# The first mixture's second layer, with an expert's slots along the columns

## The chip, the cores and the metric

The kernel runs on one core of one Trainium2 chip. Its engines work side by side, each on its own stream of instructions: TensorE (PE; its weight loads are listed as PEld), VectorE (DVE), ScalarE (ACT), GpSimd (POOL) and SyncE (SP), which here only issues transfers. The time is the device time of one launch in microseconds, the median of several runs.

## The reference

Two layers of a recurrent model run on x of 8 sequences x 512 tokens x 128 features. Each layer computes x + s * silu(g) from xn = layernorm(x): s comes from a sequence branch, g from a mixture of experts.

- In the first layer s is a state-space block (convolution, a scan over 512 tokens with 16 states of 256 channels, a small MLP). The mixture has 24 experts and picks two per token. Capacity is 86 rows per expert in each of four groups of tokens. With combine weights w and dispatch d in {0, 1}:

```
hidden = sum_e w[s,e] * ( xn[s] @ W1[e] + b1[e] )      128 -> 512
hidden = relu(layernorm(hidden))                        one weight set per group
out    = sum_e w[s,e] * ( hidden[s] @ W2[e] + b2[e] )  512 -> 128
g      = layernorm(out + xn)
```

- In the second layer s is causal attention with 8 heads, g a mixture of 128 experts.

The change touches only the first mixture.

## The kernel before

**Slots.** The routing (`routing`, L336) gives each row that an expert takes a slot: 4 x 86 = 344 rows, kept as three tiles of 128 slots, so `SLOTS` is 384 (L29, L30). `inv[p, c, e]` holds the token of slot p of tile c, `wsl` its combine weight (0 for an empty slot). `row` holds, for a token, the two slots at which it finds its experts' rows.

**The mixture** is three loops (`mixture`, near the end of `tile_kernel`), each over experts or pairs of token tiles.

1. `expert1` (L439): per tile, gather 128 rows of xn by `inv` (GpSimd, L445), transpose them (L446), and copy the three transposes out (L448). Then per tile two products into one PSUM tile, the bias (a product of a one-hot column `pick` with `bias`, which holds b1 and b2 split into three bf16 parts, L452) and the rows times W1 (L453). ScalarE scales by `wsl` into `hs` (L454), and one store per expert writes 384 rows of 2 KB to `hs_dram` (L455).
2. `between` (L457): per token tile, two gathers from `hs_dram`, their sum, a layer norm, and a store to `hid_dram`.
3. `expert2` (L506): per tile, gather 128 rows of 512 from `hid_dram` (L512), four transposes (L515), Relu into `hgT` (L517), a bias product (L518), and four products that accumulate (L520): hidden is the stationary operand, W2 the moving one, so slots lie on the partitions of the result `po`. ScalarE scales by `wsl` into `os` (L521). One store per expert goes to `os_dram` (L522).

**Order of the work.** The mixture runs beside the state-space branch (`front`, `scan`, `back`): for 64 steps of the mixture 20 steps of the scan are put between them in the source. A scan step has VectorE scans (L612), ScalarE exponentials (L608) and 16 transposes on TensorE (L616). The framework then sets each engine's static order by its own planner, so that in the trace transposes of one tile stand among products of another. `weights` (L426) loads an expert's matrix up to three experts ahead on SP's queue. The stores `hs` and `os` are on the same queue. Gathers are issued by GpSimd. After the mixture, `after` (L524) gathers from `os_dram`, so it waits for its stores.

**Buffers.** PSUM tiles of the mixture share a pool of four banks (`ps_e`, tag "pe"). In SBUF `hg`, `hs` and `hd` share four buffers (tag "big"); `xTe`/`hgT`, `os`, `lw` and `lb` have two each.

Of the kernel before, what the change touches and what calls it, by code (L numbers as in the profile page):

```python
# [8 lines left out]
F32 = mybir.dt.float32  # L9
I32 = mybir.dt.int32  # L10
BF16 = mybir.dt.bfloat16
U32 = mybir.dt.uint32
AF = mybir.ActivationFunctionType
# [7 lines left out]
P = 128  # L21
B, L, D = 8, 512, 128
NJ = L // P
# [3 lines left out]
KC = 4  # L27
E0, C0, DH, H0 = 24, 86, 512, 4

SG, CP = 3, 128  # L30
SLOTS = SG * CP
E1, C1 = 128, 32
S1 = E1 * C1
HEADS, DHEAD = 8, 128
# [12 lines left out]
def tile_kernel(ctx: ExitStack, tc: tile.TileContext, t: dict, out: bass.AP):  # L47
    nc = tc.nc
    V, S, G, T, Q = nc.vector, nc.scalar, nc.gpsimd, nc.tensor, nc.sync
# [6 lines left out]
    def load(src, shape, name, pool=None, dtype=F32):  # L56
        tl = (pool or const).tile(list(shape), dtype, name=name, tag=name)
        Q.dma_start(tl, src)
        return tl

    ident = const.tile([P, P], F32, name="ident")
# [22 lines left out]
    xn_dram = dram.tile([NTOK, D], F32, name="xn_dram")  # L84
    xT_dram = [dram.tile([P, L], F32, name=f"xT_dram{b}") for b in range(B)]
    xd_dram = [dram.tile([DTR + 2 * DS, L], F32, name=f"xd_dram{b}") for b in range(B)]
    hs_dram = dram.tile([E0 * SLOTS, DH], F32, name="hs_dram")
    hid_dram = dram.tile([NTOK, DH], F32, name="hid_dram")
    os_dram = dram.tile([E0 * SLOTS, D], F32, name="os_dram")

# [7 lines left out]
    def bc(ap, shape):  # L98
        return ap.to_broadcast(list(shape))
# [26 lines left out]
    def gather(dst, table, idx):  # L126
        G.indirect_dma_start(dst, None, table[:, :], IOA(idx, 0))  # L127
# [29 lines left out]
    ps_m = pool(ssm, "ps_m", 2, "left", space=PSUM)  # L157
# [31 lines left out]
    inv_pool = pool(moe, "inv_pool", 1, "right")  # L189
# [1 line left out]
    wsl = inv_pool.tile([CP, SG, E0], F32, name="wsl")  # L191


    bias = inv_pool.tile([3 * 32, DH + D], BF16, name="bias")
    zero = inv_pool.tile([P, L], F32, name="zero")
    G.memset(zero, 0.0)
    pick = inv_pool.tile([3 * 32, E0], BF16, name="pick")
# [3 lines left out]
    rt = pool(rt_ctx, "rt", 1, "right")  # L201
# [93 lines left out]
    lno_w = load(t["lno_w"].partition_broadcast(P), (P, D), "lno_w", w3)  # L295
    lno_b = load(t["lno_b"].partition_broadcast(P), (P, D), "lno_b", w3)

    eb = xp.tile([3 * 32, DH + D], F32, name="eb", bufs=1)
    G.memset(eb, 0.0)
    for k in range(3):  # L300
        Q.dma_start(eb[32 * k : 32 * k + E0, 0:DH], t["eb1"])
        Q.dma_start(eb[32 * k : 32 * k + E0, DH:], t["eb2"])
    part = xp.tile([3 * 32, DH + D], BF16, name="part", bufs=1)
    for k in range(3):
        ks = slice(32 * k, 32 * k + 32)
        G.tensor_copy(part, eb)
# [112 lines left out]
            )  # L419


    def chosen(e):

        return bc(pick[:, e : e + 1], (3 * 32, CP))

    def weights(shape, source):  # L426

# [11 lines left out]
    def expert1(e, w):  # L439

        we = w(e)
        px = ps_e.tile([P, SG, CP], F32, name="px", tag="pe")
        for c in range(SG):
            xg = me.tile([CP, D], F32, name="xg", bufs=8)
            gather(xg, xn_dram, inv[:, c, e : e + 1])  # L445
            T.transpose(px[:, c, :], xg, ident[:CP, :CP])  # L446
        xT = me.tile([P, SG, CP], F32, name="xTe", tag="xTe")
        S.copy(xT, px)  # L448
        hs = me.tile([CP, SG, DH], F32, name="hs", tag="big", bufs=4)
        for c in range(SG):  # L450
            ph = ps_e.tile([CP, DH], F32, name="ph", tag="pe")
            T.matmul(ph, chosen(e), bias[:, 0:DH], start=True, stop=False)  # L452
            T.matmul(ph, xT[:, c, :], we, start=False, stop=True)  # L453
            S.activation(hs[:, c, :], ph, AF.Copy, scale=wsl[:, c, e : e + 1])  # L454
        Q.dma_start(hs_dram[e * SLOTS : (e + 1) * SLOTS, :].rearrange("(c p) f -> p c f", p=CP), hs)  # L455

    def between():  # L457


        n = 2  # L460
        pairs = [(h, b0) for h in range(H0) for b0 in range(0, B, n)]
        begun, affine = [], []

        def begin(h, b0):
            if b0 == 0:
                lw = me.tile([P, DH], F32, name="lw")
                Q.dma_start(lw, t["lnh_w"][h].partition_broadcast(P))
                lb = me.tile([P, DH], F32, name="lb")
                Q.dma_start(lb, t["lnh_b"][h].partition_broadcast(P))
                affine.append((lw, lb))  # L470
            hd = me.tile([P, n, 2, DH], F32, name="hd", tag="big", bufs=4)
            for j in range(n):
                for k in range(2):
                    gather(hd[:, j, k, :], hs_dram, row[:, h * B + b0 + j, k : k + 1])
            begun.append(hd)

        for pair in pairs[:3]:
            begin(*pair)
        for i, (h, b0) in enumerate(pairs):
            if i + 3 < len(pairs):  # L480
                begin(*pairs[i + 3])
            hd, (lw, lb) = begun[i], affine[h]
            mean = st.tile([P, n], F32, name="lnh_m")
            var = st.tile([P, n], F32, name="lnh_v")
            for j in range(n):
                V.scalar_tensor_tensor(
                    hd[:, j, 0, :], hd[:, j, 0, :], 1.0, hd[:, j, 1, :], ALU.mult, ALU.add,
                    accum_out=mean[:, j : j + 1],
                )
            V.tensor_scalar(mean, mean, -1.0 / DH, None, ALU.mult)  # L490
            for j in range(n):
                S.activation(
                    hd[:, j, 1, :], hd[:, j, 0, :], AF.Square, bias=mean[:, j : j + 1],
                    accum_out=var[:, j : j + 1],
                )
            S.activation(var, var, AF.Sqrt, bias=eps6, scale=1.0 / DH)
            V.reciprocal(var, var)
            for j in range(n):
                x = hd[:, j, 0, :]
                V.scalar_tensor_tensor(x, x, mean[:, j : j + 1], lw, ALU.add, ALU.mult)  # L500
                V.scalar_tensor_tensor(x, x, var[:, j : j + 1], lb, ALU.mult, ALU.add)
                g = order(h * B + b0 + j)
                Q.dma_start(hid_dram[g * P : (g + 1) * P, :], x)
            yield

    def expert2(e, w):  # L506
        we = w(e)
        po = ps_e.tile([CP, SG, D], F32, name="po", tag="pe")
        os = me.tile([CP, SG, D], F32, name="os", tag="o")
        hg = me.tile([CP, SG, DH], F32, name="hg", tag="big", bufs=4)  # L510
        for c in range(SG):
            gather(hg[:, c, :], hid_dram, inv[:, c, e : e + 1])  # L512
            pt = ps_e.tile([P, NJ, CP], F32, name="pht", tag="pe")
            for f in range(NJ):
                T.transpose(pt[:, f, :], hg[:, c, f * P : (f + 1) * P], ident[:CP, :CP])  # L515
            hT = me.tile([P, NJ, CP], F32, name="hgT", tag="xTe")
            S.activation(hT, pt, AF.Relu)  # L517
            T.matmul(po[:, c, :], chosen(e), bias[:, DH:], start=True, stop=False)  # L518
            for f in range(NJ):
                T.matmul(po[:, c, :], hT[:, f, :], we[:, f, :], start=False, stop=(f == NJ - 1))  # L520
            S.activation(os[:, c, :], po[:, c, :], AF.Copy, scale=wsl[:, c, e : e + 1])  # L521
        Q.dma_start(os_dram[e * SLOTS : (e + 1) * SLOTS, :].rearrange("(c p) f -> p c f", p=CP), os)  # L522

    def after(b):  # L524

# [652 lines left out]
```

## Time and profile before

| | us |
|---|---|
| median of 3 runs (1658.43 to 1661.57) | 1659.78 |
| profiled execution, its time | 1664.84 |
| profiled execution, its span | 1662.9 |
| first layer of the mixture (`expert1`) | 121 to 263 |
| normalisation (`between`) | 263 to 421 |
| second layer (`expert2`) | 421 to 604 |

| engine | busy us | share of the span | in 421 to 604 |
|---|---|---|---|
| TensorE | 1246.0 | 75% | 158.7 |
| VectorE | 1237.9 | 74% | 114.2 |
| ScalarE | 961.8 | 58% | 114.7 |
| GpSimd | 585.4 | 35% | 88.9 |

The mean granted TensorE clock is 0.87 of full speed. Busy time of TensorE is the sum of matmul lengths as recorded; matmuls overlap, so starts are the better measure of pace. The chain of work that ended last passes through many engines (VectorE 33%, TensorE 33%, DMA 11%, GpSimd 10% of the span).

### The profile page before, as it was taken

How to read it: one execution, taken by the hardware profiler on the slowest of the kernel's cores; microseconds unless marked ns; L12 is line 12 of the kernel's file. 1: busy time of each engine (PE TensorE's matmuls, PEld its weight loads, DVE VectorE, ACT ScalarE, POOL GpSimd, SP SyncE). 2: the span in 40 equal slices, each digit the busy share in tenths (PEclk: the TensorE clock that was granted, in tenths of full speed). 3: DMA queues.
4: the chain of work that ended last, by engine and by line, in shares of the span. 5: the costliest groups of instructions: out<-in, count | busy, mean ns of one | idle time of the engine just before them, and what ended most of it. 6: DMA issues, size and time to landing. Idle time of an engine off the chain costs nothing.

```text
span 1662.9 us, 20509 instructions
## 1 busy us (share of the span) xinstructions
PE 1246.0 (75%) x6797; PEld 870.4 (52%) x6797; DVE 1237.9 (74%) x2809; ACT 961.8 (58%) x1691; POOL 585.4 (35%) x502
## 2 busy tenths in 40 slices
PE   4788887501599874497779987887798898889763
PEld 2644444301587872254636664575476676567442
DVE  6558766578636863699979996999999999375454
ACT  2227666666367754555766676657676675552442
POOL 2005773553653537025250232215331102020365
PEclk9887998755799985688999998999899999999986
DMA  4438987766685742223232213223231120338143
GB/s 136 148 108 261 317 308 259 240 227 202 204 280 167 249 135 55 88 77 88 83 78 70 76 51 78 90 81 85 83 95 63 59 89 13 92 102 250 54 116 96
DMA packets 170668, 222.76 MB, mean 134 GB/s; under 512 B 15722, under 2 KB 115898, under 8 KB 170562
## 3 DMA queue, kind: packets, MB, share of 16 engines
q1 hardware_dynamic: 125634, 101.35, 19.5%
q0 software_dynamic: 26496, 52.98, 12.0%
q10 hardware_dynamic: 18432, 67.12, 12.0%
q8 instruction: 54, 0.88, 0.2%
q14 instruction: 52, 0.43, 0.1%
HBM read 163.52 MB, written 57.80 MB: 133 GB/s over the span
## 4 chain that ended last, share of the span: by engine, by line
DVE 33%; PE 33%; DMA 11%; POOL 10%; issue 8%; ACT 4%; another core or an unknown queue 1%; SPq 0%; POOLq 0%; DVEq 0%; ACTq 0%
DVE u L612 8%; PE sc L835 4%; PE po L862 4%; DVE u L613 3%; DVE u L610 3%; PE ph L453 3%; DVE sc L837 3%; POOL o L130 3%; DMA hd<-hs_dram,row 2%; PE py L616 2%; PE po L520 2%; DVE s L873 2%; PE pc L556 2%; POOL hd L127 2%; PE pv L820 2%
## 5 line engine op out<-in xcount | busy, mean ns | idle before, releaser
L612 DVE TENSOR_TENSOR_SCAN u<-da,u 128x512 f32<-128x512 f32 x256 | 308.7, 1228 | 14.7 <-ACT da L608 14.2
L616 PE MATMUL py<-ident,u 128*128 128x128 f32 x1024 | 163.8, 298 | 138.2 <-DVE u L613 136.9
L616 PEld LDWEIGHTS py<-ident,u 128*128 128x128 f32 x1024 | 131.8, 154 | 178.6 <-DVE u L613 155.2
L862 PE MATMUL po<-v,pT 128*128 128x129 f32 x1280 | 184.5, 288 | 37.7 <-DVE s L873 25.8
L862 PEld LDWEIGHTS po<-v,pT 128*128 128x128 f32 x1280 | 168.5, 201 | 70.4 <-issue 42.1
L608 ACT ACTIVATE da<-dt,a_neg 128x512 f32<-128x512 f32 x256 | 177.4, 722 | 46.2 <-DVE u L612 39.7
L835 PE MATMUL sc<-xaT,qm 128*128 128x128 f32 (+3 forms) x512 | 181.5, 459 | 24.2 <-ACT prob L841 17.2
L841 ACT ACTIVATE prob<-sc,mn 128x128 f32<-128x128 f32 (+3 forms) x256 | 131.2, 529 | 117.0 <-DVE mn L837 103.4
L610 DVE TENSOR_TENSOR u<-bb,lp 128x1024 f32<-128x1024 f32 x128 | 155.3, 1230 | 44.2 <-PE py L616 17.1
L613 DVE TENSOR_TENSOR u<-u,cb 128x1024 f32<-128x1024 f32 x128 | 158.8, 1240 | 1.9 <-DMA cb<-xd_dram 0.8
L837 DVE CUSTOM_DVE_ANT_0 sc<-sc,mask 128x128 f32<-128x128 f32 (+3 forms) x256 | 124.5, 495 | 34.2 <-PE sc L835 21.8
L809 POOL DMA_INDIRECT xs_dram<-xn,idx x64 | 78.7, 1230 | 177.8 <-DVE row L806 118.6
L855 PE MATMUL pp<-ident,prob 128*128 128x128 f32 x640 | 111.3, 282 | 31.3 <-DVE pT L857 23.8
L127 POOL DMA_INDIRECT xg<-xn_dram,inv x72 | 90.0, 1249 | 121.5 <-DVE lp L578 80.2
L130 POOL DMA_INDIRECT o<-os_dram,row x64 | 115.3, 1802 | 48.9 <-DMA o<-xn_dram 28.9
L855 PEld LDWEIGHTS pp<-ident,prob 128*128 128x128 f32 x640 | 78.8, 143 | 85.1 <-DVE pT L857 28.8
L127 POOL DMA_INDIRECT hg<-hid_dram,inv x72 | 87.5, 1216 | 96.2 <-PE pht L515 50.4
L835 PEld LDWEIGHTS sc<-xaT,qm 128*128 128x128 f32 x512 | 82.9, 197 | 70.7 <-ACT prob L841 37.4
L127 POOL DMA_INDIRECT hd<-hs_dram,row x64 | 74.2, 1159 | 66.4 <-ACT zT L667 20.6
L857 ACT COPY pT<-pp 128x384 f32<-128x384 f32 (+1 forms) x115 | 59.4, 517 | 59.0 <-PE pp L855 49.9
L520 PE MATMUL po<-we,hgT 128*128 128x128 f32 x576 | 79.2, 288 | 0.2 <-ACT hgT L517 0.2
L556 PE MATMUL pc<-xT,in_cw 128*128 128x512 f32 x128 | 67.5, 679 | 13.7 <-DVE zm L680 13.7
(293 smaller groups left out, 2566.0 us busy)
## 6 DMA issues: line engine op xcount, KB each, us to landing
bb<-xd_dram ACTq DMA_DIRECT2D x64, 512.0 KB
cb<-xd_dram ACTq DMA_DIRECT2D x64, 512.0 KB
hs_dram<-hs SPq DMA_DIRECT2D x24, 768.0 KB
we<-in_W SPq DMA_DIRECT2D x48, 256.0 KB
hid_dram<-hd SPq DMA_DIRECT2D x32, 256.0 KB
we<-in_we SPq DMA_DIRECT2D x16, 512.0 KB
os_dram<-os SPq DMA_DIRECT2D x24, 192.0 KB
xb<-in_x SPq DMA_DIRECT2D x16, 256.0 KB
```

Source lines behind the costliest of these rows:

```text
L127: G.indirect_dma_start(dst, None, table[:, :], IOA(idx, 0))
L130: G.indirect_dma_start(dst, None, table[:, :], IOA(idx, 0), compute_op=ALU.add)
L608: S.activation(da[:, j, :], dt[:, hf, :], AF.Exp, scale=a_neg[:, hf, n0 + j : n0 + j + 1])
L610: V.tensor_tensor(u, bb, bc(dx[:, hf : hf + 1, :], (P, NC, L)), ALU.mult)
L612: V.tensor_tensor_scan(u[:, j, :], da[:, j, :], u[:, j, :], 0.0, ALU.mult, ALU.add)
L613: V.tensor_tensor(u, u, cb, ALU.mult)
L616: T.matmul(py[:, i, hf * P : (hf + 1) * P], u[:, j, i * P : (i + 1) * P], ident, is_transpose=True, start=False, stop=(n0 + j == DS - 1), ...
L835: T.matmul(sc[:, :w], qm[:, i * P : w], xaT[:, :w], start=True, stop=True)
L837: V.tensor_tensor_reduce(sc[:, :w], sc[:, :w], mask[:, L - w :], -1.0, FMAX, ALU.add, ALU.min, mn[:, i : i + 1])
L841: S.activation(pr, sc[:, :w], AF.Exp, bias=mn[:, i : i + 1], scale=-1.0)
L855: T.transpose(pp[:, c, :], prob[i][:, k * P : (k + 1) * P], ident)
L862: T.matmul(po[:, i - i0, :], pT[:, i * (i + 1) // 2 + k, :], v[:, k, hd % 4, :], start=(k == 0), stop=(k == i),)
```

## The change

Two things change in the first mixture.

- **Slots.** An expert's three tiles have 128, 128 and 96 rows (`SROWS`), 352 slots for 344 rows. Gathers, transposes, products and scalings of the third tile work on 96 rows; each store becomes two transfers (`store`), one of 256 rows and one of 96.
- **The second layer.** All three tiles are gathered, transposed and passed through Relu into one `hgT` of 352 columns per row block. Then four products with W2 stationary and `hgT` moving give `po` with the 128 output features on the partitions and the 352 slots along the columns. ScalarE adds the bias b2 per partition (function Identity, operand `bias2`), three transposes bring the slots back onto the partitions, and ScalarE scales by `wsl`. The bias product of this layer is gone, and so is b2's part of `bias`; `bias2` is made once at the start by loading b2, a transpose and a copy. The buffers of `oT` and `os` are those of `lw` and `lb`.

```diff
-SG, CP = 3, 128
-SLOTS = SG * CP
+CP = 128
+SROWS = (128, 128, 96)
+SG, SLOTS = len(SROWS), sum(SROWS)
...
-    bias = inv_pool.tile([3 * 32, DH + D], BF16, name="bias")
+    bias = inv_pool.tile([3 * 32, DH], BF16, name="bias")
+    bias2 = inv_pool.tile([P, E0], F32, name="bias2")
...
     for k in range(3):
-        Q.dma_start(eb[32 * k : 32 * k + E0, 0:DH], t["eb1"])
-        Q.dma_start(eb[32 * k : 32 * k + E0, DH:], t["eb2"])
+        Q.dma_start(eb[32 * k : 32 * k + E0, :], t["eb1"])
+    eb2 = load(t["eb2"], (E0, D), "eb2", rt)
+    pw = ps_m.tile([P, E0], F32, name="pb2", tag="pm")
+    T.transpose(pw, eb2, ident[:E0, :E0])
+    S.copy(bias2, pw)
...
+    def store(table, e, src):
+        r = table[e * SLOTS : (e + 1) * SLOTS, :]
+        Q.dma_start(r[: 2 * CP, :].rearrange("(c p) f -> p c f", p=CP), src[:, 0:2, :])
+        Q.dma_start(r[2 * CP :, :], src[: SROWS[2], 2, :])
...
     def expert1(e, w):
-        for c in range(SG):
+        for c, r in enumerate(SROWS):
             xg = me.tile([CP, D], F32, name="xg", bufs=8)
-            gather(xg, xn_dram, inv[:, c, e : e + 1])
-            T.transpose(px[:, c, :], xg, ident[:CP, :CP])
+            gather(xg[:r], xn_dram, inv[:r, c, e : e + 1])
+            T.transpose(px[:, c * CP : c * CP + r], xg[:r], ident[:r, :r])
...
-        Q.dma_start(hs_dram[e * SLOTS : (e + 1) * SLOTS, :].rearrange("(c p) f -> p c f", p=CP), hs)
+        store(hs_dram, e, hs)
...
     def expert2(e, w):
         we = w(e)
-        po = ps_e.tile([CP, SG, D], F32, name="po", tag="pe")
-        os = me.tile([CP, SG, D], F32, name="os", tag="o")
         hg = me.tile([CP, SG, DH], F32, name="hg", tag="big", bufs=4)
-        for c in range(SG):
-            gather(hg[:, c, :], hid_dram, inv[:, c, e : e + 1])
+        hT = me.tile([P, NJ, SLOTS], F32, name="hgT", tag="xTe")
+        for c, r in enumerate(SROWS):
+            gather(hg[:r, c, :], hid_dram, inv[:r, c, e : e + 1])
             pt = ps_e.tile([P, NJ, CP], F32, name="pht", tag="pe")
             for f in range(NJ):
-                T.transpose(pt[:, f, :], hg[:, c, f * P : (f + 1) * P], ident[:CP, :CP])
-            hT = me.tile([P, NJ, CP], F32, name="hgT", tag="xTe")
-            S.activation(hT, pt, AF.Relu)
-            T.matmul(po[:, c, :], chosen(e), bias[:, DH:], start=True, stop=False)
-            for f in range(NJ):
-                T.matmul(po[:, c, :], hT[:, f, :], we[:, f, :], start=False, stop=(f == NJ - 1))
-            S.activation(os[:, c, :], po[:, c, :], AF.Copy, scale=wsl[:, c, e : e + 1])
-        Q.dma_start(os_dram[e * SLOTS : (e + 1) * SLOTS, :].rearrange("(c p) f -> p c f", p=CP), os)
+                T.transpose(pt[:, f, :r], hg[:r, c, f * P : (f + 1) * P], ident[:r, :r])
+            S.activation(hT[:, :, c * CP : c * CP + r], pt[:, :, :r], AF.Relu)
+        po = ps_e.tile([P, SLOTS], F32, name="po", tag="pe")
+        for f in range(NJ):
+            T.matmul(po, we[:, f, :], hT[:, f, :], start=(f == 0), stop=(f == NJ - 1))
+        oT = me.tile([P, SLOTS], F32, name="oT", tag="lw")
+        S.activation(oT, po, AF.Identity, bias=bias2[:, e : e + 1])
+        pt = ps_e.tile([CP, SG, D], F32, name="pot", tag="pe")
+        os = me.tile([CP, SG, D], F32, name="os", tag="lb")
+        for c, r in enumerate(SROWS):
+            T.transpose(pt[:r, c, :], oT[:, c * CP : c * CP + r], ident)
+            S.activation(os[:r, c, :], pt[:r, c, :], AF.Copy, scale=wsl[:r, c, e : e + 1])
+        store(os_dram, e, os)
```

## The prediction

> **What bounds the kernel now.** I read the page first, then the busy time by stage, then the groups, the waits and the order of time inside the two stages that the change touches. The page has no single bound: TensorE 75% and VectorE 74% of the span. So the stages count. They are: first layer of the mixture 121 to 263 us, the normalisation from 263 to 421, second layer 421 to 604. Busy time of each engine in stretches of them (length; then PE, PEld, DVE, ACT, POOL, granted clock, DMA share, GB/s):
>
> ```profile
> 166.00:208.00 42.00, 37.76 (x155) 20.92 (x154) 32.34 (x28) 26.50 (x46) 31.68 (x24) 0.96 0.90 317
> 461.00:510.00 49.00, 45.45 (x396) 42.85 (x395) 14.71 (x13) 28.97 (x65) 27.87 (x27) 1.00 0.83 269
> 553.00:604.00 51.00, 46.73 (x396) 44.71 (x394) 42.60 (x38) 32.68 (x70) 18.65 (x15) 0.97 0.70 231
> ```
>
> In both stretches of the second layer TensorE is at 92%, at full clock: it sets the pace, with VectorE (84%) next in the later one. In the first layer the DMA engines are at 0.90. One expert of the second layer on TensorE, in order of time (start, length, engine, line, operation, shapes, count):
>
> ```profile
> 586.82 0.22 PE L518 MATMUL po<-bias,pick 96*128 96x128 bf16 x1
> 586.87 2.00 PE L520 MATMUL po<-we,hgT 128*128 128x128 f32 x16
> 588.71 0.93 PE L515 MATMUL pht<-ident,hg 128*128 128x128 f32 x7
> 589.52 0.22 PE L518 MATMUL po<-bias,pick 96*128 96x128 bf16 x1
> 589.58 1.11 PE L520 MATMUL po<-we,hgT 128*128 128x128 f32 x8
> 590.52 0.27 PE L515 MATMUL pht<-ident,hg 128*128 128x128 f32 x1
> 590.63 0.22 PE L518 MATMUL po<-bias,pick 96*128 96x128 bf16 x1
> 590.69 0.61 PE L515 MATMUL pht<-ident,hg 128*128 128x128 f32 x4
> 591.14 0.82 PE L616 MATMUL py<-ident,u 128*128 128x128 f32 x6
> 591.79 0.22 PE L518 MATMUL po<-bias,pick 96*128 96x128 bf16 x1
> ```
>
> From start to start TensorE never pauses: 16 passes take 1.84 us (115 ns each), 8 take 0.94, a transpose 110 ns, a bias product 60 ns. So an expert is 24 x 0.116 + 12 x 0.110 + 3 x 0.06 + 6 scan transposes x 0.11 = 4.95 us, and the first and last line stand 4.97 apart.
>
> **The change part by part.**
>
> *Products with slots along the columns.* A product is recorded as two passes (576 for 288). 24 passes of 128 columns become 8 of 352. No row has 352; the nearest is the first layer's pass of 512 columns, six of which take 2.58 us on the chain:
>
> ```profile
> 255.56 2.58 PE ph L453 x6
> ```
>
> That is 0.43 us, or 0.84 ns a column: 8 x 352 x 0.84 = 2.37 us against 24 x 0.116 = 2.78, so **-0.41** us. Here the Trainium skill differs (TensorE: Matmul & The Clock Gate, Back-to-back issue gap): about N / 2.4 + 2.5 ns for a warm matmul, some 81 ns for a weight load and matmul of 128. By it 24 x 81 = 1.94 us would become 8 x 149 = 1.19, a gain of 0.75, and the sum below would be about 6 us better. The f32 rows run at twice that price a column, so I take the row.
>
> *Bias products* go: 3 x 0.06 = -0.18. *Transposes of the result* come: 3 x 0.11 = +0.33. The third tile of 96 rows leaves its four transposes at 0.11, since each still loads 128 weight columns (four such loads take 0.42 us in the trace); bounds 0 and 4 x 0.03. TensorE per expert: -0.41 - 0.18 + 0.33 = **-0.26 us**. About 19 of 24 experts run at TensorE's pace (9.4 in 461 to 510, 9 or so in 553 to 604): **-4.9**. For the others, which wait on the first gathers (421 to 461) or lie in the other branch's long block (510 to 553), I count nothing.
>
> *ScalarE.* The groups (busy us, mean ns | idle before), the first four of the second layer, the last of the first layer:
>
> ```profile
> L520 PE MATMUL po<-we,hgT 128*128 128x128 f32 x576 | 79.2, 288 | 0.2 <-ACT hgT L517 0.2
> ...
> L515 PE MATMUL pht<-ident,hg 128*128 128x128 f32 x288 | 45.8, 286 | 12.5 <-DMA hg<-hid_dram,inv 10.0 <-issue 2.5
> L517 ACT ACTIVATE hgT<-pht 128x512 f32<-128x512 f32 x72 | 41.9, 598 | 5.4 <-PE pht L515 4.9
> ...
> L521 ACT ACTIVATE os<-po,wsl 128x128 f32<-128x128 f32 x72 | 26.5, 370 | 54.4 <-PE po L520 32.7 <-remote 6.7 <-PE pht L515 5.9
> ...
> L454 ACT ACTIVATE hs<-ph,wsl 128x512 f32<-128x512 f32 x72 | 48.0, 688 | 33.2 <-PE ph L453 31.9 <-DVE u L610 0.7 <-issue 0.5
> ```
>
> The new bias step is one ACTIVATE of 352 elements with a per-partition operand. Between 370 ns at 128 and 688 at 512 that is 370 + 224 x 0.83 = 555 ns. The third Relu shrinks from 512 to 384 elements, -0.11. So ScalarE has 2.90 us per expert before and 2.90 - 0.11 + 0.555 = 3.35 after, +10.7 us in all on an engine with 115 of 183 us busy. The skill speaks against putting it there (ScalarE: Activation LUTs, Rules for kernel authors): add and multiply belong on VectorE. By the row VectorE takes 0.69 us for a two-input 512 from PSUM (L680) and is the fuller engine in 553 to 604 (42.6 against 32.7), so moving it would relieve ScalarE of 0.55 and load the engine with less room; by the rule those 10.7 us would be a plain loss, by the trace most are cover.
>
> What is not free is the **order**. Before, each tile was scaled from its own products. After, products wait for all three Relus, the bias step for all products, the three transposes for the bias step, three scalings (1.11 us) for these. A handover there and back costs 0.16 (the last pass lasts 272 ns but spaces 110) + 0.06 + 0.555 + 0.05 = 0.82 us, in which TensorE needs other work: the next expert's transposes (1.32) and the scan's (0.66). These 1.98 us also have to cover the Relu of the third tile (0.16 + 0.06 + 0.49 + 0.05 = 0.76). 1.58 under 1.98: it fits, but with scaling and the scan's exponentials (0.67 each) in front on ScalarE not always. Bounds: nothing, and all of 0.82 x 24 = +19.7. Nearest to a covered wait is the same engine pair before, where each Relu was covered, so I take **+3**. Queued behind a late bias step are the next Relus on ScalarE, and behind its transposes the next products on TensorE.
>
> *Buffers.* PSUM has four banks for five tiles an expert (three transposes, result, transposed result; before four); the transposed result holds one for 1.11 us more. I put that in the +3. The output tile has two buffers, and before it was taken when an expert's first tile was scaled. There it once waited for a store (waits in 553 to 604: us in total, times, longest):
>
> ```profile
> ACT os L521 <- DMA os_dram<-os: 4.3, 2, 3.6
> ...
> PE po L518 <- ACT os L521: 3.9, 1, 3.9
> ```
>
> All three scalings now come at an expert's end, some 3.3 us later after that store, so this stall goes: **-3.9** (bounds 0 and -4.9; the late store may then hold nothing).
>
> *Tail.* Products of the last expert are no longer done tile by tile. After its last pass come the handover 0.82, transposes 0.33 and three scalings 1.11 instead of one of 0.37, then a second store issue 0.39: **+2.3**, as the gathers of the next stage wait for that store.
>
> *Third tile of 96 rows, and stores in two parts.* Per expert the first layer writes 704 KB for 768 and gathers 176 for 192: 24 x 80 KB = 2.0 MB of the 42.9 MB that this stage moves, 4.6%. If the DMA engines bounded all 142 us that is -6.5; if only TensorE did, 0. The chain there shows waits on transfers (gathers 8.9 and 6.5 us, a broadcast 7.0, a weight load 4.8) between stretches of back-to-back products, so about half: **-3.5**. In the second layer gathers shrink by 64 KB each expert; the waits on gathers at its start (10.0 us in the row of L515) by 8%: **-0.9**. POOL's gathers are 0.95 us each; fewer rows make that 0.71 to 0.95, off the path. SP's queue gets 48 more issues of 0.37 to 0.39 us; behind each stands at most a weight load wanted three experts later.
>
> *Start.* Two loads fewer on SP, POOL's four bias helpers on 512 instead of 640 columns, one transpose and one copy added: all under a microsecond beside TensorE's routing work; 0.
>
> **Sum:** -4.9 + 3 - 3.9 + 2.3 - 3.5 - 0.9 = **-7.9**. The profiled execution has a span of 1662.9 and a time of 1664.84, 5.1 above the median 1659.78; 1664.84 becomes 1656.9, and the median **1651.9**.
>
> **Rivals.**
> *All covered.* The +3 is nothing and the first layer gains its whole 6.5: -13.9, so 1645.9. For it: DMA at 0.90 there. Against it: 0.96 in its last 14 us with TensorE back to back.
> *Cancelled.* The exposure eats the rest: without it the sum is -10.9, so about 0.45 us uncovered per expert gives 1659.8. For it: 1.58 of 1.98 is little room.
> *Handover uncovered (slower).* Place: between the bias step and the three transposes, each expert, when the next expert's transposes have run already while TensorE waited for the third Relu. Price 0.82 x 24 = 19.7, so +8.8: 1668.6. It decides from 0.45 us per expert on. For it: ScalarE has 3.35 + 0.83 (1.25 exponentials of 0.67) of a 4.7 us cycle. Against it: gathers run up to four experts ahead, so transposes of the next-but-one expert exist if a bank is free.
> *Function table.* The bias step's function, Identity, is not in the trace. Relu and Copy load no table between exponentials there, and the skill (ScalarE: Activation LUTs, Table sets) has the cheap functions, identity too, in every set; no run shows it. If it were not so, two loads of 1.28 us each expert, 61 us, mostly on TensorE's wait: about 1700.
>
> **How the numbers follow.** Likeliest 42%, own range 1647 to 1656; all covered 22% (1638 to 1647); cancelled 14%; uncovered 19% (1664 to 1680); table 3%. A measurement of this kernel can tell 0.2%, 3.3 us. Faster 0.64, same 0.14, slower 0.22. The range leaves out the lower part of the covered case and the upper part of the last two: 1638 to 1671.
>
> **What would show it.** Right: eight passes of 352 columns in 2.3 to 2.5 us; second-layer stores 4.7 us apart in steady state; no wait of the scalings on a store; first layer ended 2 to 6 us earlier. Wrong: TensorE idle on the bias step or the third Relu above 0.45 us per expert, table loads beside the bias step, or passes at a price other than 0.84 ns a column. A later stage whose order comes out differently could move the end by some microseconds either way.

## The result: slower by 0.3%, where 0.5% faster was forecast

The changed kernel takes 1663.78 us (median of 20 runs, 1653.38 to 1674.03) beside 1658.2 us of the kernel before: ratio **1.0028**, interval 1.0011 to 1.0046. In a later series of runs it stood at 1.0038 (1.0018 to 1.0059). So it costs about 5 us; the forecast was a gain of 7.9. The profiled execution of the changed kernel has a time of 1663.25 and a span of 1661.2. It comes out 1.7 us under the span shown before, because that one execution of the kernel before lay 5 to 7 us above its medians (1659.78 in the first three runs, 1658.2 in 20): the pair of profiles shows where work moved, the timed runs show the 5 us.

Busy time in the same three stretches of the changed kernel (length; PE, PEld, DVE, ACT, POOL, granted clock, DMA share, GB/s):

```profile
166.00:208.00 42.00, 37.97 (x153) 20.25 (x152) 32.31 (x28) 27.83 (x48) 30.00 (x26) 0.96 0.94 313
461.00:510.00 49.00, 48.13 (x227) 30.95 (x226) 24.91 (x26) 42.02 (x79) 19.85 (x18) 0.95 0.66 200
553.00:604.00 51.00, 42.35 (x250) 31.58 (x249) 33.64 (x33) 39.05 (x79) 18.87 (x16) 0.97 0.61 180
```

The second layer now loads ScalarE nearly as much as TensorE (39 and 42 of 51 us in the last line, before 33 and 47), and DMA share fell from 0.83 and 0.70 to 0.66 and 0.61: fewer experts pass per microsecond. From its first Relu to its last scaling the second layer lasts from 415.5 to 630.7, 215 us instead of 176; an expert's stores stand 8.5 us apart in the median, before 5.4. In 415 to 631 the scan also gets further: 27.25 of its 64 steps are done at the end of the second layer, 25 before.

TensorE in order of time, around one expert (start, length, engine, line, operation; in brackets the idle time before and what ended it):

```profile
584.28 0.33 PE L532 MATMUL pot<-ident,oT 128*128 128x128 f32 x1 [1.19 <-ACT oT L528]
584.44 1.37 PE L522 MATMUL pht<-ident,hg 128*128 128x128 f32 x12
585.65 0.60 PE L677 MATMUL pzt<-ident,zm 128*128 128x128 f32 x4
586.57 0.33 PE L532 MATMUL pot<-ident,oT 128*128 128x128 f32 x1 [0.31 <-ACT da L620]
587.35 0.32 PE L532 MATMUL pot<-ident,oT 128*96 128x128 f32 x1 [0.46 <-ACT os L533]
588.83 0.44 PE L628 MATMUL py<-ident,u 128*128 128x128 f32 x2 [1.16 <-DVE u L625]
589.11 4.22 PE L526 MATMUL po<-hgT,we 128*128 128x352 f32 x8
```

TensorE waits for the bias step (L528), for ScalarE work in front of a scaling (L620), and for a scaling (L533). Before, in the rows of one expert, it had no pause. The eight passes run at a granted clock of 0.57 here (mean of 589 to 593) and last 4.06 us to the next start; at full clock six of them take 1.77 (598.53 to 600.30), 0.84 ns a column as forecast.

The groups of the new second layer (busy us, mean ns | idle before it):

```profile
L526 PE MATMUL po<-hgT,we 128*128 128x352 f32 x192 | 69.9, 512 | 5.5 <-ACT hgT L523 4.7 <-issue 0.8
...
L532 PE MATMUL pot<-ident,oT 128*128 128x128 f32 x48 | 14.1, 294 | 6.1 <-ACT oT L528 3.0 <-issue 2.4 <-ACT da L620 0.6
L528 ACT ACTIVATE oT<-po,bias 128x352 f32<-128x352 f32 x24 | 13.2, 548 | 22.3 <-PE po L526 18.8 <-PE py L604 2.2 <-issue 1.3
```

The bias step takes 548 ns (estimate 555). TensorE idles 5.5 us before products and 6.1 before full-size result transposes; with the 96-row one (1.6) that is 13.1 us, 0.55 per expert.

ScalarE also swaps its function tables more often in this stage. The costliest group of such loads in the second layer, before and after (both are for the scan's exponentials):

```profile
L608 ACT ACT_TABLE_LOAD x4 | 5.1, 1283 | 0.1
```

```profile
L620 ACT ACT_TABLE_LOAD x13 | 16.7, 1283 | 0.2
```

Between first Relu and last scaling there are 9 loads before and 27 after, all of them for functions of the state-space branch: 18 more at 1.28 us, 23 us of ScalarE. In the whole kernel there are 175 and 190.

### The profile page after: what moved, and what is told of

Same layout as the page of the kernel before. It is cut to its first block, busy times and chain, and to the rows that moved or that the text cites. A ratio compares the mean times of both kernels' runs of the same rounds, so it can differ in the third digit from the quotient of the medians.

```text
span 1661.2 us, 19808 instructions
## 1 busy us (share of the span) xinstructions
PE 1243.9 (75%) x6414; PEld 845.0 (51%) x6414; DVE 1249.6 (75%) x2813; ACT 984.9 (59%) x1727; POOL 582.6 (35%) x502
## 4 chain that ended last, share of the span: by engine, by line
PE 34%; DVE 32%; issue 9%; DMA 8%; POOL 8%; ACT 6%; another core or an unknown queue 2%; SPq 0%; POOLq 0%; DVEq 0%; ACTq 0%
DVE u L624 8%; PE sc L847 4%; DVE u L625 4%; PE po L874 3%; DVE u L622 3%; PE ph L460 3%; DVE sc L849 3%; PE py L628 3%; POOL o L131 3%; PE po L526 3%; DMA hd<-hs_dram,row 2%; PE pqm L839 2%; DVE s L885 2%; PE pc L568 2%; PE pv L832 2%
## 5 line engine op out<-in xcount | busy, mean ns | idle before, releaser
L624 DVE TENSOR_TENSOR_SCAN u<-da,u 128x512 f32<-128x512 f32 x256 | 314.7, 1248 | 66.5 <-ACT da L620 54.6
L628 PE MATMUL py<-ident,u 128*128 128x128 f32 x1024 | 169.1, 303 | 174.9 <-DVE u L625 173.1
L847 PE MATMUL sc<-xaT,qm 128*128 128x128 f32 (+3 forms) x512 | 186.1, 471 | 25.6 <-ACT prob L853 20.4
L620 ACT ACTIVATE da<-dt,a_neg 128x512 f32<-128x512 f32 x256 | 175.6, 719 | 31.8 <-DVE u L624 30.0
L131 POOL DMA_INDIRECT o<-os_dram,row x64 | 123.3, 1926 | 85.8 <-DMA os_dram<-os 42.2
L867 PE MATMUL pp<-ident,prob 128*128 128x128 f32 x640 | 113.7, 287 | 34.7 <-DVE pT L869 24.2
L128 POOL DMA_INDIRECT xg<-xn_dram,inv x72 | 84.3, 1171 | 126.6 <-DMA wsl<-wsl_h 81.0
L832 PE MATMUL pv<-w_vo,xaT 128*128 128x512 f32 x128 | 73.1, 669 | 6.3 <-DVE zm L692 4.1
L829 POOL MEMSET v<- 128x16 f32 x16 | 3.9, 284 | 208.5 <-PE po L874 163.2
```

The source lines that it names most:

```text
L131: G.indirect_dma_start(dst, None, table[:, :], IOA(idx, 0), compute_op=ALU.add)
L620: S.activation(da[:, j, :], dt[:, hf, :], AF.Exp, scale=a_neg[:, hf, n0 + j : n0 + j + 1])
L624: V.tensor_tensor_scan(u[:, j, :], da[:, j, :], u[:, j, :], 0.0, ALU.mult, ALU.add)
L628: T.matmul(py[:, i, hf * P : (hf + 1) * P], u[:, j, i * P : (i + 1) * P], ident, is_transpose=True, start=False, stop=(n0 + j == DS - 1), ...
L847: T.matmul(sc[:, :w], qm[:, i * P : w], xaT[:, :w], start=True, stop=True)
L867: T.transpose(pp[:, c, :], prob[i][:, k * P : (k + 1) * P], ident)
```

## The experiments

The runs were made in several series, and only ratios to the kernel before in the same series are compared: it took 1634.0 us in the first (this section's first two parts) and 1657 to 1659 in the later ones. Why is not known; both traces of the whole kernel from the first series are shorter at the very end, from head 48 to 64 of the attention (206 and 207 us; 221 to 232 in all others). Scan steps are counted in VectorE's stream, heads (64 in all) by the attention's exponentials on ScalarE.

### One part of the change at a time

The first run takes the slots, with the old second layer and its bias product. The second takes the new second layer and its bias, with three tiles of 128 rows.

```diff
# slots alone, on the kernel before
-SG, CP = 3, 128
+SROWS = (128, 128, 96)
# second layer alone, on the changed kernel
-SROWS = (128, 128, 96)
+SROWS = (128, 128, 128)
```

> Only the third tile of 96 rows and the stores in two parts; the second layer as before. Theory 1 (the second layer's longer chain between TensorE and ScalarE costs, the slots help): 3 to 8 us faster than the kernel before, ratio 0.995 to 0.998. Theory 2 (the slots and the doubled stores cost, or shift the start of later stages badly): 2 to 6 us slower, ratio 1.001 to 1.004. Second layer, first Relu to last scaling, by theory 1 about as before (176 us in the profile).

Measured: 1626.26 us, ratio **0.9956** (0.9942 to 0.9969), as the first theory had it.

> Only the second layer with slots along the columns, in three tiles of 128 and one store. Theory 1: 7 to 12 us slower than the kernel before, ratio 1.004 to 1.007, and the second layer again over 200 us long. Theory 2: ratio 0.996 to 1.000, and the second layer under 185 us.

Measured: 1607.73 us, ratio **0.9854** (0.9833 to 0.9875). The second layer is 210.9 us long, as expected, and the kernel is nevertheless the fastest of these. Both parts gain singly, and together they lose: the parts don't add, so a sum over them cannot be the whole story. (The changed kernel itself was not run in this first series; its 1.0028 and 1.0038 come from others.) The theory that the longer second layer is what costs fell with this run: at the end of head 18 it is level with the run of slots alone (940 us in both traces), at the end of head 20 it is 16 us ahead (992 for 1007).

### The first mixture with nothing beside it

Scan, attention and second mixture are left out of both kernels; the mixture's result is written out. What remains is an expert's own pace (one execution each).

> Leaves out the scan branch, the attention, the second mixture and its weights; only routing, the first mixture and its combination, as in the kernel before. A reference for the next run: the second layer at TensorE's pace without the scan's transposes, about 4.3 us per expert, 24 x 4.3 + 8 for the first gathers = 111 us.

> The same parts left out, with the mixture of the changed kernel. If the wait of TensorE on the bias step and the third Relu is covered by the next expert's transposes, 24 x 4.05 + 8 + 2 = 107 us for the second layer. If the whole handover of 0.82 us stays open, 24 x 4.9 + 10 = 127 us. If only the mixing with the scan branch makes it slow (theory 1b), it is as fast alone as the old form or faster.

Measured: second layer 117.4 us unchanged, 156.1 changed; in steady state about 4.65 and **6.25 us** per expert, the latter outside all that was expected. TensorE unchanged, then changed:

```profile
420.96 0.22 PE L518 MATMUL po<-bias,pick 96*128 96x128 bf16 x1
421.02 0.50 PE L515 MATMUL pht<-ident,hg 128*128 128x128 f32 x3
421.48 0.22 PE L518 MATMUL po<-bias,pick 96*128 96x128 bf16 x1
421.53 2.00 PE L520 MATMUL po<-we,hgT 128*128 128x128 f32 x16
```

```profile
441.78 2.63 PE L526 MATMUL po<-hgT,we 128*128 128x352 f32 x8 [0.83 <-ACT hgT L523]
445.12 0.33 PE L532 MATMUL pot<-ident,oT 128*128 128x128 f32 x1 [0.71 <-ACT oT L528]
445.29 0.60 PE L522 MATMUL pht<-ident,hg 128*128 128x128 f32 x4
...
448.04 2.63 PE L526 MATMUL po<-hgT,we 128*128 128x352 f32 x8 [0.83 <-ACT hgT L523]
```

Two waits per expert, 0.83 for the third Relu and 0.71 for the bias step, are 1.54 of the 1.6 us. ScalarE in the same expert:

```profile
444.52 0.55 ACT L528 ACTIVATE oT<-po,bias 128x352 f32<-128x352 f32 x1 [2.78 <-PE po L526]
445.49 0.37 ACT L533 ACTIVATE os<-pot,wsl 128x128 f32<-128x128 f32 x1 [0.42 <-PE pot L532]
```

It stands still for 2.78 us while the products run, and then TensorE stands still for it.

### What sets 6.25 us

Two edits of the changed second layer, in the form with nothing beside it. In the first the three transposes of a result stand ahead of its three scalings (all three share a PSUM bank); in the second the gathers, transposes and Relus of the next expert are also emitted ahead of this expert's products.

```diff
         for c, r in enumerate(SROWS):
             T.transpose(pt[:r, c, :], oT[:, c * CP : c * CP + r], ident)
+        for c, r in enumerate(SROWS):
             S.activation(os[:r, c, :], pt[:r, c, :], AF.Copy, scale=wsl[:r, c, e : e + 1])
# second edit, with expert2 split at hT
+        hT = inputs2(0)
         for e in range(E0):
-            expert2(e, w)
+            following = inputs2(e + 1) if e + 1 < E0 else None
+            expert2(e, w, hT)
+            hT = following
```

> The changed kernel's first mixture with nothing beside it (scan, attention and second mixture left out), with the three transposes of a result written ahead of its three scalings. In the same form the unchanged second layer took 4.65 us per expert and the changed one 6.25. If the exchange in one bank is the larger part of the 1.6 us: 5.2 to 5.6 us per expert. If the waits for the bias step and for the third Relu are the larger part: 5.7 to 6.2 us.

> The changed first mixture with nothing beside it (scan, attention and second mixture left out), transposes written ahead of the scalings, and an expert's gathers, transposes and Relus emitted one expert ahead of its products. If products and ScalarE took turns (2.63 us of products, then 3.4 us of ScalarE and the handovers between): PE then has 1.37 + 2.63 + 0.55 and one wait of 0.7 for the bias step, 5.0 to 5.5 us per expert instead of 6.25. If something else sets the pace (gathers, the stores, the banks): 5.8 to 6.4 us.

Measured: 6.25 us per expert with the first edit (the 0.83 for the third Relu became 1.16), **4.90** with both; each is a little off the ranges expected, and 4.90 is still more than the old form's 4.65. TensorE with both:

```profile
439.73 1.37 PE L521 MATMUL pht<-ident,hg 128*128 128x128 f32 x12
440.94 2.60 PE L530 MATMUL po<-hgT,we 128*128 128x352 f32 x8
444.25 0.55 PE L536 MATMUL pot<-ident,oT 128*128 128x128 f32 x3 [0.71 <-ACT oT L532]
```

The exchange in one bank was not the cause. TensorE and ScalarE took turns: with all products of an expert in one block, the next expert's Relus came behind this one's bias step and scalings. Emitted one expert ahead they run under the products, the wait for the third Relu is gone, and only the 0.71 for the bias step is left.

### The mixture and the scan, without attention

This pair leaves out attention and second mixture, and with them most of what the planner could lay out differently behind the first mixture; the rest of the scan is left.

> The kernel before without attention and without the second mixture: only the prologue, the first mixture with the scan beside it, the rest of the scan, and the mixture's outputs, which are written out as the result. What it leaves out is everything that the planner could lay out differently behind the first mixture. Theory 1 (the second layer's gaps are filled with scan work): the end of the scan is the end of the run, for both kernels of this pair. Both theories expect the second layer at 160 to 190 us here.

> The changed kernel with the same parts left out (attention, second mixture). Theory 1 (the gaps are filled; the scan is 2 to 3 steps further when the second layer ends, and what the prologue, the first layer and the bias save is kept): the second layer is 25 to 45 us longer, and yet the scan ends 5 to 40 us earlier than in the unchanged kernel of this pair. Theory 2 (the handovers cost something that no scan work takes up): the scan ends 0 to 30 us later.

Measured: 1224.54 us unchanged, **1209.52** changed, one execution each, with spans of 1222.8 and 1207.8. Busy time from 421 to 604, first unchanged, then changed:

```profile
421.00:604.00 183.00, 158.25 (x1212) 141.61 (x1212) 113.36 (x107) 114.95 (x231) 89.36 (x74) 0.94 0.68 219
```

```profile
421.00:604.00 183.00, 155.44 (x853) 113.16 (x851) 121.00 (x116) 136.91 (x267) 81.84 (x69) 0.95 0.67 207
```

The second layer ends at 626.7 instead of 602.5, 24.2 us later. But the scan is 2.25 steps further by then, and what is left of it takes 431.8 us (626.7 to 1058.5) instead of 472.1 (602.5 to 1074.6): its end is 16.1 us earlier, the span 15.0. TensorE in the second layer of this pair is idle 29 us instead of 20, counted from start to start, and occupied 182 instead of 156: since the mixture's own matmuls didn't grow (106 us for 112), the 26 us are work of the scan branch. So without attention the changed kernel is **faster by 15 us**: 12.6 of them are there when `between` ends (404.0 for 416.6), 2.4 come behind that. Single executions of the unchanged whole kernel scatter from 1652 to 1667 us, so the 2.4 can't be told from nothing. The theory that the handovers cost something of their own expected the end 0 to 30 us later; it came earlier. A cost of a few microseconds behind `between` isn't ruled out by one pair, one of 19.7 is not seen.

### The plan behind the mixture

The new second layer alone, at 0.9854, differed from the changed kernel between heads 18 and 20, where VectorE waits in the kernel before for the gathers of the mixture's output 5. Waits and busy time of the kernel before in these two heads:

```profile
POOL zm L679 <- PE pzt L665: 21.2, 1, 21.2
DVE lno_st L106 <- DMA o<-os_dram,row: 12.3, 4, 9.3
```

```profile
962.00:1030.00 68.00, 51.31 (x233) 31.42 (x232) 49.59 (x103) 43.93 (x79) 24.27 (x13) 0.87 0.26 64
```

The changed kernel has the same stall (69 us, 955 to 1024); the fast one had 52 us. So the theory was: the place of these gathers decides. One call in the source, moved two heads forward, brings them forward in both kernels, and gives both the same order of POOL from output 3 on:

```diff
+                if hd == 1 and b == 1:
+                    ahead = after(b + 1)
                 if hd == 3:
-                    ready[b + 1] = beside.prepare(b + 1, after(b + 1))
+                    ready[b + 1] = beside.prepare(b + 1, ahead if b == 1 else after(b + 1))
```

> The changed kernel once more, beside the three others of this call, so that they are compared on one chip. Both theories expect the ratio of the result again, 1.001 to 1.005 of the kernel before, a second layer of some 215 us, and PE idle between heads 18 and 20 of the attention branch while VectorE waits for the gathers of output 5. If the ratio comes out under 0.995 instead, the chip and not the program decides, and neither theory stands.

> The kernel before, with one call moved: the mixture's output for batch 2 is emitted two heads earlier (at head 1 of batch 1 instead of head 3). No work is added or left out. In the planned order of POOL the normalisation of output 3 then comes before the gathers of output 4, and the gathers of output 5 some 8 scatters earlier, as in the run with the new second layer alone. Theory 1 (the end is decided by where the planner puts the gathers during attention): ratio 0.985 to 0.993, the idle of VectorE before the statistics of output 5 falls from 7 to 9 us to under 1 us, heads 18 to 20 last under 60 us instead of 67 to 69. Theory 2 (the second layer itself made the run with it alone fast): ratio 0.998 to 1.002, since the second layer is the old one.

> The changed kernel with the same call moved (the output of batch 2 emitted at head 1 of batch 1 instead of head 3), nothing added or left out; POOL's planned order in the attention part is then the same as in the kernel before with that call moved. Theory 1 (order of the gathers): ratio 0.978 to 0.990, within 0.6% of the other kernel with the moved call, although its second layer is still some 210 us long. Theory 2 (the changed kernel is slow because its second layer is 39 us longer): ratio 1.000 to 1.005, over 0.8% above the other kernel with the moved call.

Measured: 1.0038 (1.0018 to 1.0059) as given, **1.0041** (1.0021 to 1.0060) for the kernel before with the moved call, 1.0013 (0.9986 to 1.0039) for the changed one. VectorE's wait for output 5 is gone in both (0.0 us before its statistics), and neither kernel is at 0.99. Heads 6 to 16 take 157 and 158 us where they took 146 in both: the stall moved forward. This theory, in the form that one place decides, fell too.

The same series had the transposes of a result ahead of the scalings, in the whole kernel:

> The changed kernel, with the three transposes of an expert's result written ahead of the three scalings, so that none of them waits for a scaling of the tile before in the same bank. Same work. Theory 1: the second layer gets shorter by the exchange, 24 x (0.3 to 0.8) = 7 to 19 us (196 to 208 us), and since the planner here also puts the normalisation of output 3 ahead of the gathers of output 4, the ratio is 0.980 to 0.990. Theory 2 (the length of the second layer goes to the end one to one): ratio 1.0028 less 7 to 19 us of 1660, 0.991 to 0.999.

Measured: **0.9909** (0.9881 to 0.9938). The second layer is 204.4 us long instead of 212.0 (beside it, as given), and heads 18 to 20 take 52 us:

```profile
949.00:1001.00 52.00, 48.06 (x260) 32.13 (x259) 51.11 (x99) 41.86 (x82) 3.11 (x1) 1.00 0.21 66
```

VectorE does 51.11 us of work in 52 here, beside 49.59 in 68 before. An edit that gains nothing with the mixture alone (6.25 again) gains 1.3% on the changed kernel beside it (0.9909 for 1.0038). Most of it stands where the plan came out differently: the profile is 6 us ahead of the changed kernel's at the end of head 18 (949 for 955) and 23 at the end of head 20 (1001 for 1024).

### Changed and unchanged under two other plans

If the plan decides, the change has to be measured under several. The constant that says how many scan steps are emitted beside the mixture is changed in both kernels; the work stays.

```diff
-    MIX = 20
+    MIX = 19
```

> The kernel before with one constant of the interleaving changed: 19 instead of 20 steps of the scan are emitted beside the first mixture, so the planner lays out the rest differently. No work is added or left out. This and the three other runs of the call are a pair of pairs: the change itself (new second layer, 96 rows, bias) under two other plans. Theory 1 (the longer second layer is filled with scan work and gives nothing net, and the end moves with the plan of the attention part by as much as the change is worth): the four ratios spread over 1% or more, and the two ratios of changed to unchanged kernel under the same constant differ by over 0.5% from each other, with a mean under 1.000. Theory 2 (the change costs 0.3 to 0.4% by its own handovers, whatever the plan): changed to unchanged is 1.001 to 1.006 in both pairs. For this run: theory 1 0.985 to 1.01, theory 2 0.997 to 1.003.

> The changed kernel with 19 instead of 20 steps of the scan emitted beside the first mixture, nothing added or left out. Theory 1: anywhere from 0.985 to 1.005, and its ratio to the unchanged kernel with 19 steps is not 1.0033. Theory 2: 1.001 to 1.006 times the unchanged kernel with 19 steps. Both expect a second layer of 195 to 225 us, 30 to 45 us longer than in the unchanged kernel with 19 steps.

> The kernel before with 21 instead of 20 steps of the scan emitted beside the first mixture, nothing added or left out. Theory 1: 0.985 to 1.01. Theory 2: 0.997 to 1.003.

> The changed kernel with 21 instead of 20 steps of the scan emitted beside the first mixture, nothing added or left out. In its planned order the normalisation of output 3 comes directly behind that of output 2, ahead of the gathers of output 4, as in the two fast runs so far (new second layer alone, transposes ahead of the scalings). If that place is what makes a plan fast: 0.983 to 0.992. Theory 2: 1.001 to 1.006 times the unchanged kernel with 21 steps.

| plan | unchanged | changed | changed to unchanged |
|---|---|---|---|
| as given | 1 | 1.0028 and 1.0038 | 1.003 |
| call moved | 1.0041 | 1.0013 | 0.997 |
| 19 steps | 1.0268 (1.0230 to 1.0306) | 0.9982 (0.9963 to 1.0002) | 0.972 |
| 21 steps | 0.9897 (0.9852 to 0.9943) | 0.9881 (0.9845 to 0.9916) | 0.998 |

The last column is a quotient of the two before it. The unchanged kernel moves by 3.7% over four plans of the same work; most of that is the plan with 19 steps, whose 1.0268 lies outside what either theory expected (0.985 to 1.01). The change is worth +0.3% to -2.8%, and only the plan as given shows a loss beyond its interval. A cost of the change of its own, 1.001 to 1.006 under every plan, is refuted by the pair with 19 steps. With 21 steps alone it would not be: combined, the intervals of that pair reach from about 0.992 to 1.004.

The table loads don't order these plans: the unchanged kernel with 19 steps, the slowest, has 174, the changed one with 21 steps 180, the one with the transposes first 188. What the 15 more loads of the changed kernel cost was not tried singly.

### Do a good plan and the repaired handover add up?

> The changed kernel with the transposes written ahead of the scalings and with 21 instead of 20 steps of the scan emitted beside the first mixture, nothing added or left out. If what the two edits gave singly (1.2% and 1.5% of the changed kernel) were two separate savings they would add up: 0.974 to 0.980. Theory 1 (both did the same thing, they moved the plan to a good one, and the shorter handover itself is worth little beside the scan): 0.984 to 0.992.

> The changed kernel with the transposes written ahead of the scalings and an expert's gathers, transposes and Relus emitted one expert ahead of its products; nothing added or left out. Theory 1 (the gaps in the second layer are filled with scan work anyway, and the plan behind it decides): the second layer is 10 to 30 us shorter than the 212 to 215 us, the scan about as much less far at its end, and the ratio lies where the plans so far put it, 0.985 to 1.003. Theory 2 (the shorter second layer goes to the end): 1.0033 less 10 to 30 us of 1660, 0.985 to 0.997, and the scan no less far than 27.25 steps when the second layer ends.

Measured: **0.9861** (0.9812 to 0.9909) for the transposes first with 21 steps, so the two gains don't add. The pipelined second layer (both edits above) in the whole kernel stands at **0.9853** (0.9813 to 0.9893), 1634.25 us beside 1657.94: it beats both kernels as given. Its second layer is 170.9 us long, 41 to 44 shorter than in the changed kernel, and the scan is 24.25 steps far at its end instead of 27.25. With fewer gaps in the second layer, less scan work is done during it: how long that stage lasts says nothing alone about the end.

## Why the prediction was wrong

**Products with slots along the columns: the price was right, a lower clock took part of the saving.** A column costs 0.84 ns, and with nothing beside them an expert's eight passes take 2.63 us from the first start to the modelled end of the last. In the whole kernel each product is counted from its start to the next start and no longer than its own length. So counted, 19 of the 24 experts ran at full clock and occupy TensorE for 2.47 us each, 0.1 over the forecast's 2.37; five ran at a mean granted clock of 0.56 to 0.75 and occupy it for 3.97 each. That makes 66.8 us, 2.78 per expert. In the kernel with the transposes first only two experts are slow, and the same products occupy 60.6 us. (The Trainium skill's formula that the forecast weighed, in TensorE: Matmul & The Clock Gate, Back-to-back issue gap, is for an isolated matmul, and the page itself says that it counts too much for long ones; for a pass of 352 it gives an estimate of 149 ns. The passes here space 295 ns at full clock, so the row was the one to take.) Result transposes are 0.48 per expert (11.5 us) instead of 0.33, as they come one at a time behind waits. Transposes of 96 rows start 82 ns apart where those of 128 rows start 109 apart: the forecast put this at nothing for the sake of the weight load, and it is 0.11 per expert, its bound. With the input transposes (32.1 us, before 37.6) the new layer occupies TensorE 110.4 us; the old one had 37.6 + 70.6 and 72 bias products of 0.06, 112.5. So -0.09 us per expert in place of -0.26. (Two sums of the forecast are 0.1 us too large: 9.4 and 9 experts are 18.4 and not 19, and 8% of 10.0 us is 0.8.)

**ScalarE and the function: right, with a term missing.** 548 ns, and no table load belongs to the bias step. With nothing beside the mixture both kernels load 20 tables in all. The function-table rival is out. But beside the scan the stage has 18 loads more, 23 us of ScalarE where the forecast added 10.7 in all; in the whole kernel it is 15 loads more, 19 us.

**The order: +3, mis-sized in place and wrong in what it reaches.** "1.58 under 1.98: it fits" failed. The 1.98 us of cover were there, but ScalarE had to do the next Relus behind this expert's bias step and scalings, so cover and work came one after the other. With nothing beside it TensorE waits 1.54 us an expert, the second layer is 38.7 us longer, and in the whole kernel TensorE waits 13.1 us (0.55 per expert, over the 0.45 named as the sign of a wrong forecast). That is the rival "handover uncovered", whose 1668.6 is also nearest to what was measured. That is luck: its price doesn't reach the end by the way it named, since with scan work in the gaps the pair without attention ends 15 us earlier.

**Buffers, -3.9: the wait went.** No scaling waits for a store of the mixture in the changed kernel. In a stage that is 39 us longer its 3.9 us can't be seen.

**Tail, +2.3: mis-sized.** From the end of the last expert's last product to GpSimd's first gather for the next stage it takes 10.6 us (622.45 to 633.09), before 4.2 (602.84 to 607.03): +6.4. Three of ScalarE's table loads, 3.8 us, stand between that expert's bias step and its last scaling. Only the last step is no longer: 2.4 us from the last scaling to the gather, before 3.8. On a stage end that moved by 27 us this decides nothing.

**Third tile of 96 rows and the start: too small together.** For `between` to end took 418.3, 420.2 and 416.6 us in the three unchanged profiles with the constant 20, and 405.4, 408.6, 409.2, 408.5, 404.8 and 404.0 in six changed ones, 14 scan steps done in all. The means are 418.4 and 406.8, -11.6 instead of -3.5 + 0. Some of it is the start, put at 0: with nothing beside it the first scaling of the first layer comes at 132.1 instead of 138.6. In the whole kernel it comes 2.7 us earlier in the mean of the same profiles (140.4 for 143.1), and GpSimd's helpers for the bias begin at 23.7 us instead of 32.2. How the rest is split isn't settled; slots alone and second layer alone both reach about 408 here, too, so the parts overlap. Nor is it the same under every plan: with 21 steps the gain at this point is 7.3 us (407.0 for 414.3), with 19 steps 4.6 (402.9 for 407.5, with 12.5 and 13.25 scan steps done), one profile each. The whole slots edit is worth 0.4%, where the sum gave it 4.4 us, 0.3%.

**The sum: the failing step.** It added what each edit saves or costs in its own stage, and took the total to the end. Without attention the sign comes out right, -15 for -7.9 forecast, but by luck: most of it is the start and `between`, and the second layer, forecast to be shorter, is 37 us longer. Then the planner lays out the rest of the scan and 64 heads anew behind a mixture that ends 27 us later with the scan 2.25 steps further. The forecast gave this one sentence, "some microseconds either way", and no size. Measured, it is 55 us between the medians of the best and the worst plan of the unchanged kernel (1643.86 and 1699.18; 0.9897 to 1.0268 of the plan as given). In the plan as given the change loses about 16 us behind `between`, from -11.6 to +5. What in that plan eats them is only partly seen: at the end of head 16 the changed profile is 11 us ahead (929 for 940), at head 20 and 40 it is 6 ahead (1024 for 1030, 1324 for 1330), at head 48 3 (1409 for 1412). So most of the lead outlives the second layer by 300 us and is lost from head 16 on; the second profile of the changed kernel has the same ends to within 3 us (930, 1024, 1321, 1407). The rest lies within the scatter of single executions, and one profile of the kernel before, itself 5 us above its median, can't place it. That is left open.

**What of the rivals:** "all covered" failed in place but not at the end of the pair without attention; "cancelled" gave 1659.8, and 1663.8 is measured. The range of 1638 to 1671 held; its sign and middle did not.

## What to carry to other kernels

Where two branches share a core and a planner fills one's gaps with the other, the length of a stage says little: ask how far the other branch is when the stage ends, and cut the program behind both (here: without attention) before a stage is blamed or praised. When a change of half a percent is measured under one static order, measure the unchanged kernel under two or three other orders of the same work first; here they spread over 3.7%. When small products become one block, emit the next item's inputs ahead of it, or the engine that feeds them and TensorE will take turns (6.25 us an expert; 4.90 with the inputs one expert ahead; 4.65 in small products).

## What the runs showed of the hardware

- The same eight passes took 2.37 us at full clock and 4.06 us at a granted clock of 0.57. Idle time of TensorE just before does not tell which: of two blocks of passes in the changed kernel, the first started behind 10 us in which TensorE was busy for 9.96 and ran at 0.61, the second behind 10 us with 6.14 busy and ran at full clock. What lowers the clock was not tried. (Busy time by stretch as above, each time the 10 us ahead of the passes and the passes.)

```profile
496.60:506.60 10.00, 9.96 (x42) 4.82 (x41) 5.09 (x6) 9.87 (x19) 4.00 (x4) 1.00 0.60 169
506.60:510.60 4.00, 4.00 (x9) 2.24 (x9) 2.02 (x2) 2.77 (x5) 2.23 (x3) 0.61 0.54 146
```

```profile
555.10:565.10 10.00, 6.14 (x41) 4.66 (x40) 8.15 (x7) 7.56 (x15) 3.80 (x4) 1.00 0.58 172
565.10:567.60 2.50, 2.50 (x11) 1.60 (x10) 2.25 (x2) 1.75 (x2) 0.91 (x1) 1.00 0.75 210
```

- Input transposes of 96 rows start 82 ns apart, those of 128 rows 109 ns (medians in the changed kernel; both load 128 weight columns).
- VectorE's 128x128 normalisation in the prologue takes 345 ns in the middle and up to 2061 ns (1817 in the changed kernel). The long ones stand beside GpSimd's elementwise work for the bias, which the change cut from 640 to 512 columns; the link is argued, not shown. (The Trainium skill, GPSIMD Engine Reference, Specifications, has GpSimd's SBUF interfaces shared with VectorE, with contention where a VectorE instruction has two SBUF inputs or runs in a mode that uses two ports; whether this one does, no run here shows, and none took GpSimd's work away.)
